# Linear attention and a mixture of experts in one kernel: the issue order of SyncE's loads, GpSimd's transfers and two groups of TensorE work

## The chip, the cores and the metric

The kernel runs on one core of one Trainium2 chip. The metric is the device time of one execution in microseconds (us), as the median of several runs. A core has five engines, each with its own instruction queue that it works through in order: TensorE (PE; its weight loads are shown as PEld), VectorE (DVE), ScalarE (ACT), GpSimd (POOL) and SyncE (SP, which only issues transfers here). Transfers issued by SyncE and by GpSimd run on the core's 16 DMA engines.

## The reference, cut to what matters

```
x: [4, 2048, 256], so 8192 tokens of 256
xn = layernorm(x)
# attention: 8 heads, keys of 128, values of 64, a gated linear recurrence
q, k, v = xn Wq, xn Wk / sqrt(128), xn Wv
alpha   = sigmoid((xn Wg + bg) / 16)            # one per token and head
state   = alpha * state + outer(k, v)           # over the tokens of a sequence
att     = ((q . state) * sigmoid(xn Wog)) Wo
# experts: 64, of which each token takes 8, at most 256 tokens an expert
scores  = sigmoid(xn gate_w^T)
groups  = the best 4 of 8 groups of 8 experts, by their two best (scores + bias)
top 8   = the best 8 experts in them; weights = 2.5 * scores / their sum
buf[e]  = the first 256 tokens that chose e
y       = (silu(buf w_gate) * (buf w_up)) w_down            # for each expert
ffn     = for each token the weighted sum of its experts' y
out     = x + att + ffn
```

## The kernel before

The work has two strands that are interleaved on all engines.

**Attention** runs over 32 blocks of 256 tokens (`block(s)`). Every product is made of three half-precision products of high and low parts (`product`, L253 to L257: high x high, high x low, low x high). A block loads its transposed tokens `xs`, its decay rows `aj` and `mv` and its decay factors `el` (`load_block`, `load_el`), all one block ahead. It projects them (`project`, tile `pj`: `queries`, `keys`, `values`, `gate`), splits the results into parts on ScalarE (L206) and VectorE (L207), and has the keys of four heads at a time transposed by a DMA from SyncE (`kt`, L841, two of them in a block). `unit_a` makes the scores and decays `sp` and `dc`, `unit_m` multiplies them (L874), `unit_d` makes outputs and the new state (`od`, which reads `kt`), `output` multiplies by Wo, and `finish(s - 1)` adds the block before to the output: by one accumulating transfer from GpSimd (L940), and for the last two blocks through SyncE: read, add on VectorE, write (L945 to L948).

**The experts' strand** first routes: 16 batches of 512 tokens. `front` normalizes them, stores them, has them transposed (`xT`, L366, a DMA from SyncE on what GpSimd leaves at L363), and four calls later makes the logits `lg` (L378 to L382). `back` chooses the experts and counts. When all batches are routed (about 605 us), the experts begin, at 5 for each 12 steps of the attention:

- `steps(g)` loads the counts of NF experts (`c`, L557) and subtracts them (L560), and `find` makes of them the row numbers `idx` of an expert's 256 tokens, three experts ahead;
- `fetch(e)` loads the expert's weights `w` (three transfers of 128 KB from SyncE, L589 to L591) and gathers its tokens `xe` (two indirect transfers from GpSimd, L594);
- `expert_in` transposes the tokens on TensorE (`xet`, L607) and splits weights (`wh` on ScalarE, L611, `wl` on VectorE, L679) and tokens;
- `expert_mid` makes `gu`, `expert_out` makes `yp` and `y` (L651);
- `expert_add` adds `y` to the output rows (two indirect accumulating transfers from GpSimd, L665). Each waits until the last two additions, or a block's finish between them, have landed (`behind_adds`).

```
        new = owed[0] >= 1.0                      # at 5 of 12 steps
        ...
    for it in list(q):                            # expert_step: every expert in flight, one stage on
        expert_stages[st](e, m)
    ...
    moe["at"].append([e, fetch(e), 0])            # then the next expert's transfers
```

So an expert is gathered in one period (2.4 steps) and transposed in the next; its additions are written in the fourth period after its gather, just ahead of the gather of the expert four later. `block` calls `step()` 12 times, in the last block 7 times, 379 in all; the experts begin at the 205th step, and the last of the 64 gathers is written at about the 358th.

**What sets the order.** The source order is not the issue order. The kernel is compiled with a scheduler that gives each engine the instruction it holds to be ready first, and the earlier written among several; it estimates for itself how long transfers take. The order is fixed in the program, so an engine that comes to an instruction too early waits. `tc.issue_after(ins)` puts what is written in its block behind `ins` in the queue of the same engine; it orders the issue alone and waits for nothing.

## Time and profile before

| | |
|---|---|
| median of 3 runs | 1246.25 us (1245.57 to 1248.66) |
| profiled execution | 1258.39 us, of which its span is 1256.6 us |
| granted TensorE clock, mean | 0.982 |
| TensorE busy, 60 to 560 us (routing and attention) | 466.4 of 500 us |
| TensorE busy, 600 to 1240 us (experts and attention) | 602.9 of 640 us |
| DMA, mean over the span | 162 GB/s |

The profile is of one execution. Its page gives the busy time of each engine, then groups of instructions by line, engine and tile; tiles are named as in the kernel, `out<-in`. A row of a waits view reads "engine, line waited for, what ended the wait: us in total, times, longest". A row of a timeline gives start, duration, engine, line, operation, count, and in brackets the engine's idle time before it and what ended that. SPq is SyncE issuing a transfer; the time beside it is that of the issue, not of the transfer. The chain is the work that ended last, followed back to the start; a DMA piece in it runs from issue to landing.

### The profile page before, as it was taken

Reading aid. Unit: us, or ns where it says so; the run is one execution under the profiler, and the core shown is the slowest. Engines: PE = TensorE matmul, PEld = TensorE weight load, DVE = VectorE, ACT = ScalarE, POOL = GpSimd, SP = SyncE. Lnnn points to the kernel's source line nnn. Section 1 sums busy time; section 2 is a strip of 40 time slices with the busy share of each in tenths; the row PEclk is TensorE's granted clock in tenths of the full one; section 3 lists DMA queues with packets and bytes.
Section 4 is the critical chain, followed back from the end, with each engine's and each line's share of the span. In section 5 each row is a group of like instructions: output and inputs, shape, how many; then the busy total and the mean of one; then the engine's idle time right before and its main releaser. Section 6 shows DMA issues by size and latency. Waiting matters only on the chain.

```text
span 1256.6 us, 32315 instructions
## 1 busy us (share of the span) xinstructions
PE 1146.2 (91%) x12421; PEld 961.1 (76%) x12421; DVE 960.6 (76%) x2685; ACT 754.4 (60%) x1455; POOL 740.5 (59%) x961
## 2 busy tenths in 40 slices
PE   3697999999999989998999999899889999999898
PEld 2576777877777767787887888788678888787686
DVE  7986777777676767777898788787768889787676
ACT  4566666756665656655566566565556666565564
POOL 4376777665777767552356466655467566564651
PEclk9998999999999999999999999899989999999899
DMA  7649878777777776648689797898778797998854
GB/s 234 197 93 254 196 177 179 166 186 167 176 173 153 174 143 138 157 94 192 128 178 156 158 189 146 163 181 159 144 162 166 175 178 161 155 172 161 142 77 85
DMA packets 313498, 203.74 MB, mean 162 GB/s; under 512 B 198528, under 2 KB 283648, under 8 KB 313088
## 3 DMA queue, kind: packets, MB, share of 16 engines
q1 hardware_dynamic: 280608, 156.05, 53.2%
q0 software_dynamic: 32736, 45.63, 22.9%
q8 instruction: 97, 1.59, 0.5%
q14 instruction: 57, 0.47, 0.1%
HBM read 112.57 MB, written 54.71 MB: 133 GB/s over the span
## 4 chain that ended last, share of the span: by engine, by line
PE 48%; DMA 19%; DVE 12%; POOL 10%; issue 6%; ACT 4%; SPq 1%; POOLq 0%; DVEq 0%; ACTq 0%
PE pj L257 8%; PE pj L255 8%; PE pj L256 8%; DMA xe<-xw_d,idx 7%; DMA xT<-x 4%; PE od L891 3%; DMA el<-el_d 3%; PE od L895 3%; DMA kt<-k 2%; PE xet L607 2%; PE gu L255 2%; PE gu L256 2%; PE gu L257 2%; POOL out_dram L665 1%; DVE qt L822 1%
## 5 line engine op out<-in xcount | busy, mean ns | idle before, releaser
L665 POOL DMA_INDIRECT out_dram<-y,idx x128 | 210.3, 1643 | 207.0 <-ACT y L651 40.1
L594 POOL DMA_INDIRECT xe<-xw_d,idx x128 | 136.8, 1068 | 49.2 <-issue 32.3
L257 PE MATMUL pj<-xs,wk_l 128*128 128x256 f16 x496 | 135.6, 273 | 0.0
L255 PE MATMUL pj<-xs,wk_h 128*128 128x256 f16 x496 | 135.4, 273 | 0.0
L256 PE MATMUL pj<-xs,wk_h 128*128 128x256 f16 x496 | 135.3, 273 | 0.0
L256 PE MATMUL pj<-xs,wq_h 128*128 128x256 f16 x496 | 135.3, 273 | 0.0
L257 PE MATMUL pj<-xs,wq_l 128*128 128x256 f16 x496 | 135.2, 273 | 0.0
L255 PE MATMUL pj<-xs,wq_h 128*128 128x256 f16 x496 | 135.2, 273 | 0.0
L874 DVE TENSOR_TENSOR dc<-sp,dc 128x512 f32<-128x512 f32 x128 | 87.7, 685 | 57.3 <-POOL dc L861 49.8
L891 PE MATMUL od<-dc,v 128*64 128x128 f32 x1024 | 112.9, 291 | 9.5 <-DVE dc L874 8.4
L207 DVE SCALAR_TENSOR_TENSOR ql<-pj,qh 128x512 f16<-128x512 f32 x128 | 87.2, 681 | 39.4 <-ACT qh L206 39.1
L206 ACT ACTIVATE qh<-pj 128x512 f16<-128x512 f32 x128 | 76.3, 596 | 48.9 <-PE pj L257 48.5
L895 PE MATMUL od<-qt,state 128*64 128x128 f32 x960 | 103.4, 279 | 0.0
L255 PE MATMUL sp<-qh,k 128*128 128x128 f16 x512 | 96.5, 221 | 0.2 <-ACT k L206 0.2
L206 ACT ACTIVATE k<-pj 128x512 f16<-128x512 f32 x128 | 76.0, 594 | 34.4 <-PE pj L257 33.9
L256 PE MATMUL sp<-ql,k 128*128 128x128 f16 x512 | 96.1, 220 | 0.0
L257 PE MATMUL sp<-qh,k 128*128 128x128 f16 x512 | 95.5, 220 | 0.0
L855 ACT ACTIVATE dc<-lp 128x512 f32<-128x512 f32 x128 | 76.6, 599 | 28.4 <-PE lp L851 27.8
L207 DVE SCALAR_TENSOR_TENSOR k<-pj,k 128x512 f16<-128x512 f32 x128 | 86.9, 679 | 8.2 <-ACT k L206 7.9
L891 PEld LDWEIGHTS od<-dc,v 128*64 128x64 f32 x1024 | 62.0, 138 | 39.7 <-DVE dc L874 11.8
L822 DVE SCALAR_TENSOR_TENSOR qt<-pj,el 128x512 f32<-128x512 f32 x128 | 86.7, 678 | 2.1 <-DMA el<-el_d 2.1
L679 DVE TENSOR_TENSOR wl<-w,wh 128x768 fp32r<-128x768 f32 x64 | 61.1, 955 | 35.0 <-ACT wh L611 33.9
(397 smaller groups left out, 4282.9 us busy)
## 6 DMA issues: line engine op xcount, KB each, us to landing
el<-el_d SPq DMA_DIRECT2D x64, 512.0 KB
xw_d<-x SPq DMA_DIRECT2D x16, 512.0 KB
xT_d<-xT SPq DMA_DIRECT2D x16, 512.0 KB
out_dram<-in_L_attn_x_dram SPq DMA_DIRECT2D x16, 512.0 KB
w<-in_L_ffn_w_gate_dram SPq DMA_DIRECT2D x64, 128.0 KB
w<-in_L_ffn_w_up_dram SPq DMA_DIRECT2D x64, 128.0 KB
w<-in_L_ffn_w_down_dram SPq DMA_DIRECT2D x64, 128.0 KB
xs<-xT_d SPq DMA_DIRECT2D x31, 256.0 KB
```

Of the source, the lines that this page charges most:

```text
L206: return (nc.scalar.activation(hi, t, AF.Copy, scale=scale).ins, nc.vector.scalar_tensor_tensor(lo, in0=t, scalar=scale, in1=hi, op0=ALU.m ...
L207: nc.vector.scalar_tensor_tensor(lo, in0=t, scalar=scale, in1=hi, op0=ALU.mult, op1=ALU.subtract).ins)
L255: nc.tensor.matmul(out_, lhsT=a[0], rhs=b[0], start=first, stop=False)
L256: nc.tensor.matmul(out_, lhsT=a[0], rhs=b[1], start=False, stop=False)
L257: return nc.tensor.matmul(out_, lhsT=a[1], rhs=b[0], start=False, stop=last).ins
L594: nc.gpsimd.indirect_dma_start(out=xe[:, f, :], out_offset=None, in_=xw_d[:, :], in_offset=bass.IndirectOffsetOnAxis(ap=idx[:, e, f:f + 1] ...
L665: two = [nc.gpsimd.indirect_dma_start(out=of, out_offset=bass.IndirectOffsetOnAxis(ap=idx[:, e, f:f + 1], axis=0), in_=m["y"][:, f, :], in ...
L822: read = nc.vector.scalar_tensor_tensor(qt, in0=pj, scalar=QFIT, in1=two_heads(el, i), op0=ALU.mult, op1=ALU.mult)
L855: nc.scalar.activation(dc, lp, AF.Relu, scale=-1.0)
L874: anchor.append(nc.vector.tensor_tensor(dc, B["sp"], dc, ALU.mult).ins)
L891: nc.tensor.matmul(op[i * DV:(i + 1) * DV, j, :], lhsT=v[:, h0 + 2 * j + i, :], rhs=dc[:, 2 * j + i, :], start=True, stop=first)
L895: nc.tensor.matmul(op[i * DV:(i + 1) * DV, j, :], lhsT=state[half][:, 2 * j + i, :], rhs=qt[:, ck, 2 * j + i, :], start=False, stop=True)
```

## The change

- `steps`, the weights of an expert, `load_block` and `load_el` issue their SyncE transfers behind the last key transposition written so far (`behind_keys`).
- GpSimd's gathers, additions and block finishes are issued in the order in which they are written (`in_turn`).
- The logits and the experts' token transposes are issued behind the last projection written so far (`behind_projections`).
- An expert's weights become a stage of their own between gather and transposes. So the transposes and all later stages of an expert come one period later after its gather, with five token buffers in place of four.
- NF is 4 in place of 8: counts are loaded for four experts at a time.
- The last block but one is added to the output by GpSimd's accumulating transfer, like those before it.

```diff
--- before.py
+++ after.py
@@ -53,7 +53,7 @@
 DGROUPS = ((0, 1), (1, 1), (2, 2), (4, 4), (8, 4), (12, 4))
 
 STEPS = 12
-NF = 8
+NF = 4
 AHEAD = 2
 EXPERTS = 5
 
@@ -297,6 +297,10 @@
     zs = r1.tile([P, NB, H, RT], F32, name="zs")
     sg = r1.tile([P, NB, H, RT], F32, name="sg")
     batch = {}
+
+    def behind_projections():
+
+        return tc.issue_after(made["pj"]) if "pj" in made else ExitStack()
 
     def load_x(b):
         rows = slice(b * RB, (b + 1) * RB)
@@ -376,10 +380,11 @@
         for _ in range(3 if b > 2 else 1):
             yield True
         lg = ps["mo"].tile([P, RT, E + H], F32, tag="mo", name="lg")
-        for t in range(RT):
-            for c in range(2):
-                made["lg"] = product(lg[:, t, :], (xT[:, t, 0, c, :], xT[:, t, 1, c, :]),
-                                     (gwz[:, 0, c, :], gwz[:, 1, c, :]), c == 0, c == 1)
+        with behind_projections():
+            for t in range(RT):
+                for c in range(2):
+                    made["lg"] = product(lg[:, t, :], (xT[:, t, 0, c, :], xT[:, t, 1, c, :]),
+                                         (gwz[:, 0, c, :], gwz[:, 1, c, :]), c == 0, c == 1)
         nc.vector.scalar_tensor_tensor(zs[:, b].rearrange("p h t -> p t h"), in0=lg[:, :, E:E + H],
                                        scalar=unfit[:, WG:WG + 1], in1=bc(brow, 1, RT),
                                        op0=ALU.mult, op1=ALU.add)
@@ -549,13 +554,24 @@
 
     moe = {}
 
+    def in_turn(issue):
+
+        with tc.issue_after(moe["turn"]) if "turn" in moe else ExitStack():
+            moe["turn"] = issue().ins
+        return moe["turn"]
+
+    def behind_keys():
+
+        return tc.issue_after(made["kt"]) if "kt" in made else ExitStack()
+
     def steps(g):
 
         both = []
         for t in range(2):
             c = moe["m1"].tile([NTL, NF, P], F16, name=f"c{t}")
-            nc.sync.dma_start(out=c, in_=cnt_d[t * E:(t + NTL) * E, :].rearrange(
-                "(t e) i -> t e i", e=E)[:, g * NF:(g + 1) * NF, :])
+            with behind_keys():
+                nc.sync.dma_start(out=c, in_=cnt_d[t * E:(t + NTL) * E, :].rearrange(
+                    "(t e) i -> t e i", e=E)[:, g * NF:(g + 1) * NF, :])
             both.append(c)
         nc.vector.tensor_tensor(dd_t[g % 2][0:NTL, :, 0:P], both[1], both[0], ALU.subtract)
 
@@ -584,27 +600,31 @@
             find(e)
 
     def fetch(e):
-        w4 = moe["w4"]
-        w = w4.tile([P, 6, I], F32, name="w", bufs=3)
-        nc.sync.dma_start(out=w[:, 0:2], in_=w_gate[e].rearrange("(c p) i -> p c i", p=P))
-        nc.sync.dma_start(out=w[:, 2:4], in_=w_up[e].rearrange("(c p) i -> p c i", p=P))
-        nc.sync.dma_start(out=w[:, 4:6].rearrange("p c i -> p (c i)"), in_=w_down[e])
-        xe = w4.tile([P, 2, XW], F32, name="xe", bufs=4)
+        xe = moe["w4"].tile([P, 2, XW], F32, name="xe", bufs=5)
         for f in range(2):
-            nc.gpsimd.indirect_dma_start(
+            in_turn(lambda: nc.gpsimd.indirect_dma_start(
                 out=xe[:, f, :], out_offset=None, in_=xw_d[:, :],
-                in_offset=bass.IndirectOffsetOnAxis(ap=idx[:, e, f:f + 1], axis=0))
-        return dict(w=w, xe=xe)
+                in_offset=bass.IndirectOffsetOnAxis(ap=idx[:, e, f:f + 1], axis=0)))
+        return dict(xe=xe)
+
+    def expert_weights(e, m):
+        w = moe["w4"].tile([P, 6, I], F32, name="w", bufs=3)
+        with behind_keys():
+            nc.sync.dma_start(out=w[:, 0:2], in_=w_gate[e].rearrange("(c p) i -> p c i", p=P))
+            nc.sync.dma_start(out=w[:, 2:4], in_=w_up[e].rearrange("(c p) i -> p c i", p=P))
+            nc.sync.dma_start(out=w[:, 4:6].rearrange("p c i -> p (c i)"), in_=w_down[e])
+        m["w"] = w
 
     def expert_in(e, m):
 
         xt = ps["mo"].tile([P, 2, 2, 2, P], F16, tag="mo", name="xet")
-        for f in range(2):
-            rows = m["xe"][:, f, 0:D].bitcast(F16)
-            for a in range(2):
-                for c in range(2):
-                    k = (2 * a + c) * P
-                    nc.tensor.transpose(xt[:, a, c, f, :], rows[:, k:k + P], identh)
+        with behind_projections():
+            for f in range(2):
+                rows = m["xe"][:, f, 0:D].bitcast(F16)
+                for a in range(2):
+                    for c in range(2):
+                        k = (2 * a + c) * P
+                        nc.tensor.transpose(xt[:, a, c, f, :], rows[:, k:k + P], identh)
         w3, m1 = moe["w3"], moe["m1"]
         wh = w3.tile([P, 6, I], F32R, name="wh")
         wl = w3.tile([P, 6, I], F32R, name="wl")
@@ -662,16 +682,16 @@
     def expert_add(e, m):
 
 
-        two = [nc.gpsimd.indirect_dma_start(
+        two = [in_turn(lambda: nc.gpsimd.indirect_dma_start(
             out=of, out_offset=bass.IndirectOffsetOnAxis(ap=idx[:, e, f:f + 1], axis=0),
             in_=m["y"][:, f, :], in_offset=None, compute_op=ALU.add,
-            bounds_check=NT - 1, oob_is_err=False).ins for f in range(2)]
+            bounds_check=NT - 1, oob_is_err=False)) for f in range(2)]
         for ins in two:
             behind_adds(ins)
         tc.declare_no_dep(two[1], two[0], reason="the halves of an expert share no row")
         adds.extend(two)
 
-    expert_stages = [expert_in, expert_mid, expert_out, expert_add]
+    expert_stages = [expert_weights, expert_in, expert_mid, expert_out, expert_add]
 
     def expert_late():
 
@@ -688,7 +708,7 @@
             if st == len(expert_stages):
                 continue
             expert_stages[st](e, m)
-            if st == 1:
+            if st == 2:
                 mids.append((e, m))
             it[2] += 1
         for e, m in mids:
@@ -838,7 +858,7 @@
         split(two_heads(k[:, :, 0], i), two_heads(k[:, :, 1], i), pj, DK ** -0.5 * KFIT)
         if i == 1:
             kt = ktp.tile([P, NCK * 2 * 4, P], F16, name="kt")
-            nc.sync.dma_start(out=kt, in_=k.rearrange("p c a h t -> p (c a h t)"), transpose=True)
+            made["kt"] = nc.sync.dma_start(out=kt, in_=k.rearrange("p c a h t -> p (c a h t)"), transpose=True).ins
             B["kt"][half] = kt
 
     def unit_a(s, half, ck):
@@ -936,9 +956,9 @@
     def finish(s):
         res = blk[s]["res"]
         rows = slice(s * S, (s + 1) * S)
-        if s < NS - 2:
-            behind_adds(nc.gpsimd.dma_start(out=of[rows, :].rearrange("(t p) d -> p t d", p=P), in_=res,
-                                            accum_op=ALU.add).ins)
+        if s < NS - 1:
+            behind_adds(in_turn(lambda: nc.gpsimd.dma_start(
+                out=of[rows, :].rearrange("(t p) d -> p t d", p=P), in_=res, accum_op=ALU.add)))
         else:
             mo = xsp.tile([P, NCK, D], F32, tag="xs", name="mo")
             dst = of[rows, :].rearrange("(t p) d -> p t d", p=P)
@@ -953,8 +973,9 @@
 
         n = s + 1 < NS
         if n:
-            load_block(s + 1)
-            load_el(s + 1, 0)
+            with behind_keys():
+                load_block(s + 1)
+                load_el(s + 1, 0)
         unit_a(s, 0, 0)
         if n:
             queries(s, 1, 0)
@@ -984,7 +1005,8 @@
         else:
             queries(s, 1, 1)
         if n:
-            load_el(s + 1, 1)
+            with behind_keys():
+                load_el(s + 1, 1)
             gate(s + 1, 0)
         step()
         unit_d(s, 0, 1)
```

## The prediction

> **What bounds the kernel now.** I read the page first, then TensorE's waits, the busy times by stage, and the timelines of GpSimd and SyncE around the worst waits. The page, core 0:
>
> ```profile
> PE 1146.2 (91%) x12421; PEld 961.1 (76%) x12421; DVE 960.6 (76%) x2685; ACT 754.4 (60%) x1455; POOL 740.5 (59%) x961
> ```
>
> TensorE works 91% of 1256.6 us; no other engine passes 76%. So a change gains only what it takes from TensorE's 110 us of idle time, and from matmuls run at a lowered clock. Who ends the idle time (in total, times, longest, us):
>
> ```profile
> PE xet L607 <- DMA xe<-xw_d,idx: 33.4, 22, 7.2
> PE lg L255 <- DMA xT<-x: 31.1, 15, 9.8
> PE tot L171 <- ACT junk L155: 9.3, 1, 9.3
> PE od L891 <- DVE dc L874: 8.4, 9, 3.2
> PE od L255 <- DMA kt<-k: 4.5, 3, 2.8
> ```
>
> Two rows hold 64.5 us: the token transposes of an expert wait for gathered rows (expert phase, from 605 us), and the logits for transposed tokens (routing phase). From 60 us on the second is 20.9 us in 13 waits; the rest is start-up, which the change leaves alone. Transposed keys, by contrast, are waited for three times. What a long wait leaves behind, by stretch (length, PE busy, PEld, DVE, ACT, POOL, PEclk, DMA share, GB/s):
>
> ```profile
> 803.00:812.00 9.00, 6.35 (x63) 5.16 (x64) 3.02 (x12) 2.32 (x4) 6.47 (x6) 0.62 0.58 104
> 907.00:914.00 7.00, 0.00 (x0) 0.00 (x0) 1.91 (x5) 0.19 (x1) 5.11 (x4) 0.65 0.59 139
> 914.00:920.00 6.00, 5.30 (x23) 3.09 (x23) 1.72 (x4) 1.81 (x4) 4.69 (x4) 0.55 0.53 77
> ```
>
> TensorE stands still for 7 us, then works at 0.55 of its clock. How the worst wait came about, GpSimd's timeline and then TensorE's:
>
> ```profile
> 885.75 0.95 POOL L594 DMA_INDIRECT xe<-xw_d,idx  x1 [0.30 <-issue]
> 888.09 1.40 POOL L940 DMA_DIRECT2D out_dram<-res  x1
> 898.51 1.65 POOL L665 DMA_INDIRECT out_dram<-y,idx  x1 [9.02 <-DMA out_dram<-res]
> 907.24 1.55 POOL L665 DMA_INDIRECT out_dram<-y,idx  x1 [5.21 <-ACT hs L628]
> 910.96 1.02 POOL L594 DMA_INDIRECT xe<-xw_d,idx  x1 [0.30 <-issue]
> 912.28 0.98 POOL L594 DMA_INDIRECT xe<-xw_d,idx  x1 [0.30 <-issue]
> ...
> 914.19 0.61 PE L607 MATMUL xet<-identh,xe 128*128 128x128 f16 x4 [7.24 <-DMA xe<-xw_d,idx]
> ```
>
> One gather was pulled ahead of the finish of a block (L940); the next then came only behind that finish and two experts' additions, each of which waits for the landing before it: 25 us between gathers instead of 9.4 (64 experts' gathers start over 605.9 to 1202.9). TensorE reached the transposes 2 us after the second gather was issued. SyncE, with the chain's piece for its last line:
>
> ```profile
> 1059.67 0.37 SPq L764 DMA_DIRECT2D el<-el_d  x1
> 1061.29 0.34 SPq L740 DMA_DIRECT2D xs<-xT_d  x1
> 1061.76 0.37 SPq L589 DMA_DIRECT2D w<-in_L_ffn_w_gate_dram  x1
> 1063.29 5.29 SPq L841 DMA_TRANSPOSE kt<-k  x1
> ...
> 1063.29 13.29 DMA kt<-k
> ```
>
> Loads that nobody needs for another 15 us or more stand right ahead of a key transposition, which then takes 13.29 us against 6.13 and 7.51 elsewhere on the chain.
>
> **The change, part by part.**
>
> *A period later.* An expert's gather is now followed by a step for its weights, and only then by its transposes. One period is 597/63.5 = 9.4 us. The longest wait for a gather is 7.2 us, so one more period covers every one of the 22. This holds if the compiled order really sets the transposes a period further from their gather: in the trace they come 1 to 38 us after the last projection written ahead of them (only the first expert's come before it), so it is the scheduler's estimate of the gather, not the source, that places them. With four experts in flight, an expert's additions (which stand ahead of the gather four later) come about 34 us after its gather (981 to 1015), or 8.5 us an expert: just about the period, which is why the experts fall ever further behind the attention. With five in flight the same 34 us is 6.8 an expert, and the source position can rule. I take four fifths of the 33.4: -27, and keep 6 for gathers behind a block's finish. Bounds: 0 and -33.
>
> *The clock.* After the waits of 2.6, 4.1, 7.2 and 5.1 us at 690, 805, 914 and 1167 the granted clock was 0.76, 0.62, 0.55 and 0.59 over 7, 9, 6 and 6 us, with 6.8, 6.4, 5.3 and 5.6 us of busy time: lost 0.24 x 6.8 + 0.38 x 6.4 + 0.45 x 5.3 + 0.41 x 5.6 = 8.7 us. The Trainium skill ("TensorE: Matmul & The Clock Gate", "What's actually happening") has half clock follow an idle window of about 3.4 us and last about as long; that would price three waits at 1.7 each, 5 us. The trace shows a wait of 2.6 us doing it too, so I use 8.7, with the same four fifths: -7.
>
> *GpSimd in program order.* No instruction is added; the few gathers that now stand ahead of a finish or of earlier additions (646, 691, 886 and 1129 us among them) fall behind these. Such a gather is then issued up to 9.0 us (wait for the finish) plus two additions of 1.6 later. Of two periods' lead, 18.8 us, some 6 are left, against gathers of 3 to 10 us on the chain: that is the 6 us kept above. In exchange no 25 us hole follows. Queued behind are only other transfers: in this phase GpSimd computes nothing. The last-but-one block's finish goes from SyncE (0.38 + 2 x 0.36 us of issue, two VectorE additions of 0.42) to one GpSimd issue of 1.3, before the end and beside TensorE: 0.
>
> *Loads behind the last keys.* Nothing is added but their wait. They are moved past kt, and whatever is moved past it runs later: per block two el, xs, two aj, two mv, and five experts' w (three transfers each) and c. The gain: kt has the rings to itself; od's waits for it are 4.5 us in all, so at most -4. The price: what is late next. xs and el are read half a block (15 us and more) later, against 5.29 of issue and landings of 4 to 9 us; covered. The weights are the closest: written one period, 9.4 us, before ScalarE copies them (wh), and five experts against two key transpositions a block means 2 of 5, or 26, are written just behind one. The skill ("DMA: Bandwidth & Descriptors", "Two DMAs through the same engine are not ordered") says descriptors of a queue start in order: weights begin only behind kt, which speaks against this change. In the trace the three loads issued at 1070.90 behind the kt of 13.29 landed by 1077.43, 0.85 us after it and 14.1 us after its issue. By that slow kt a load would come 4.7 us late, 26 of them 122 us; by one of 7.5, 8.4 us, which is in time. By the rule without overlap (7.5 plus the 2.81 us of a w piece on the chain) it would be 0.9 late. Since kt loses the traffic ahead of it, I take the ordinary kt and +2 (bounds 0 and +122).
>
> *Logits behind the last projection.* All 15 later lg already stand 0 to 26 us behind it, so this edge moves none. What can move is xT. GpSimd waited for el before L363, which makes xT's input, 3.81 us at 229.81 (L828); that el is now issued elsewhere. Against it, the block's second el is now written next to xT. Between -20.9 and +20 (13 el pieces of 4.4 us, a third of each seen) I take -4, close to the row of kt's traffic.
>
> *Smaller steps.* NF 4: 16 more c issues of 0.52 us on SyncE and 8 more subtractions of 0.34 to 0.67 on VectorE (at most 5 us of 300 idle): 0 while VectorE stays at 76%.
>
> *The end.* Now the experts, trailing, fill TensorE until 1226:
>
> ```profile
> 560.00:600.00 40.00, 36.75 (x382) 29.61 (x382) 30.94 (x70) 21.31 (x41) 8.85 (x11) 0.96 0.66 153
> 1200.00:1240.00 40.00, 40.00 (x424) 33.96 (x424) 26.39 (x55) 22.97 (x46) 17.07 (x12) 1.00 0.59 88
> 1240.00:1257.00 17.00, 10.84 (x129) 9.08 (x126) 10.42 (x20) 5.56 (x11) 0.00 (x0) 1.00 0.24 62
> ```
>
> If they no longer trail, the last 17 of 379 steps run attention alone, some 45 us as in the first row, which loses 3.25 in 40; the last block without filler loses a little more. +5 (0 to +12).
>
> Sum: -27 - 7 - 4 + 2 + 5 = -31. The profiled execution took 1258.39 us (its span and 1.8 around it), 1% over the median of 1246.25; -31 leaves 1227 there, 1215 against the median.
>
> **The rivals.** *Just in time again.* If the scheduler goes on placing the transposes by its own estimate, they move up with their gathers and the waits stay; so would they if GpSimd's fixed order cost what the period gives. For: the order by estimate above. Against: five experts in flight. Then -5 instead of -27 and no clock gain: -5 - 4 + 2 + 5 = -2, 1244.
>
> *Weights too late (slower).* ScalarE reaches wh before the weights have landed and holds the casts of qh, k and xeh behind it, on which TensorE's buffers hang. Halfway between in time and the slow kt's 4.7, 2.4 us at each of 26 is +62: 1277. It decides from 31/26 = 1.2 us an expert on. For: kt at 13.29, and a DMA share of 0.9 at 1080 to 1120. Against: today ScalarE waits for w 5.0 us in all (three waits), and it idles 40%.
>
> **How the numbers follow.** Gain as summed: 0.58, own range 1198 to 1235. Just in time: 0.17 (0.08 faster, 0.07 same, 0.02 slower). Late weights: 0.25, 1250 to 1280. Below 0.3% (3.7 us) a measurement of this kernel can't tell a change from none. Faster 0.66, same 0.07, slower 0.27. The range: 1194 takes in most of the logits' 21 us; 1266 takes in half of the late weights; about 0.05 and 0.11 are left out.
>
> **What would show it.** Right: xet's wait for xe below 10 us; no clock under 0.9 in 40 us stretches after 605; about 9.4 us between gathers; kt pieces under 9 us; the last experts' additions ending before 1200. Wrong: xet still at 25 us or more (first rival), or ScalarE's wh waiting for w above 30 us and pj or gu among TensorE's waits (second), or lg's wait above 31.

## The result: slower by 3%

The changed kernel takes 1286.39 us (median of 4 runs, 1284.07 to 1298.42), against 1247.45 us of the kernel before on the same chip (4 runs, 1245.57 to 1256.32): ratio 1.0317, 95% interval 1.0236 to 1.0399. The forecast was 1215 us. A ratio here compares means of runs on the same chip without those more than 1.5% above the fastest of their kernel, so it can exceed the quotient of the medians, by up to 0.6% in most rows below and by 1.4% for e27, where 7 of 11 runs of the kernel before are left out. The profiled execution took 1287.55 us (span 1285.8), against 1258.39 before. The page, core 0:

```profile
PE 1157.5 (90%) x12421; PEld 969.7 (75%) x12421; DVE 958.4 (75%) x2691; ACT 753.2 (59%) x1454; POOL 750.4 (58%) x962
```

TensorE does the same 12421 matmuls and is busy 11 us longer; its idle time grew from 110 to 128 us. The two make up the 29 us between the profiled spans. The first is the clock: in both traces TensorE's granted clock is either 1.00 or 0.50, and it stood at 0.50 for 44 us before and 69 us after. What ends the idle time (TensorE's waits, the whole span):

```profile
PE lg L255 <- DMA xT<-x: 31.5, 12, 9.8
PE pj L255 <- DVE qt L842: 11.9, 6, 3.2
PE od L255 <- DMA kt<-k: 11.6, 2, 10.6
...
PE xet L627 <- DVE idx L594: 11.3, 3, 5.3
...
PE row L587 <- DVE dd L576: 6.7, 4, 2.5
```

The row that led before, `xet <- DMA xe` with 33.4 us, is gone. In its place stand waits for things that come from SyncE: row numbers and differences of counts (`idx` and `dd`, both made from `c`), and one wait of 10.6 us for transposed keys. VectorE's and ScalarE's waits show the same loads from the other side:

```profile
DVE dd L576 <- DMA c<-cnt_d: 47.0, 12, 7.0
```

```profile
ACT wh L631 <- DMA w<-in_L_ffn_w_down_dram: 22.4, 12, 4.7
```

GpSimd did what was forecast of it. Its timeline at a block's finish, where a gather once ran ahead and left a hole of 25 us:

```profile
907.39 1.01 POOL L605 DMA_INDIRECT xe<-xw_d,idx  x1 [0.30 <-issue]
908.71 1.60 POOL L605 DMA_INDIRECT xe<-xw_d,idx  x1 [0.30 <-issue]
911.00 1.37 POOL L960 DMA_DIRECT2D out_dram<-res  x1 [0.69 <-ACT dc L876]
915.62 1.76 POOL L685 DMA_INDIRECT out_dram<-y,idx  x1 [3.25 <-DMA out_dram<-res]
917.68 1.58 POOL L685 DMA_INDIRECT out_dram<-y,idx  x1 [0.30 <-DVE hs L651]
919.57 1.03 POOL L605 DMA_INDIRECT xe<-xw_d,idx  x1 [0.31 <-PE pj L257]
```

The next gather is 12 us later, and the wait for the finish to land is 3.25 us of that. From an expert's second gather to its transposes there are 17.4 us on the mean of experts 8 to 59, before 8.1.

**Where the 29 us went.** The first key transposition of a block is a good milestone: SyncE issues 64 of them, two a block. Their times in the two profiled executions, and the end of TensorE's work, with TensorE's idle time in each stretch and what half the clock cost it (half of its busy time at 0.50), before and after:

| stretch | before | after | difference | idle | half clock |
|---|---|---|---|---|---|
| start to block 16 (routing) | 569.9 | 585.1 | +15.2 | 64.3, 70.0 | 3.6, 15.9 |
| block 16 to block 19 (the experts begin) | 108.6 | 119.5 | +10.9 | 3.7, 13.1 | 1.5, 3.1 |
| block 19 to block 30 (experts) | 508.2 | 498.2 | -10.0 | 35.9, 27.3 | 10.2, 7.7 |
| block 30 to TensorE's last matmul | 66.2 | 79.1 | +12.9 | 2.8, 14.0 | 0.0, 2.2 |

So a third of the forecast gain is there, in the middle; three losses stand around it. The first is more clock than waiting, the other two are waits. SyncE stands long at key transpositions in all three. Its timeline where the experts begin:

```profile
599.68 1.00 SPq L784 DMA_DIRECT2D el<-el_d  x1
611.25 1.81 SPq L861 DMA_TRANSPOSE kt<-k  x1
613.11 1.76 SPq L573 DMA_DIRECT2D c<-cnt_d  x2
...
619.33 0.44 SPq L613 DMA_DIRECT2D w<-in_L_ffn_w_gate_dram  x1
```

From 600.7 to 611.25 SyncE issues nothing: the transposition waits for its keys, and the counts, a block's loads and weights stand behind it. The first counts go out at 613.11. In the kernel before they go out some 40 us earlier:

```profile
568.70 0.52 SPq L557 DMA_DIRECT2D c<-cnt_d  x1
573.60 0.58 SPq L557 DMA_DIRECT2D c<-cnt_d  x1
```

The first gather is at 623.4, before at 605.9. At the end:

```profile
1253.12 0.38 SPq L965 DMA_DIRECT2D mo<-out_dram  x1
1253.60 9.57 SPq L861 DMA_TRANSPOSE kt<-k  x2
```

The last block's read of the output (L965) waits for the last additions, and here it stands ahead of the last two key transpositions. TensorE waits 10.6 us for them. SyncE's wait there:

```profile
SPq L965 <- DMA out_dram<-y,idx: 20.0, 1, 20.0
```

Busy times by stage of the kernel after (length, PE busy, PEld, DVE, ACT, POOL, PEclk, DMA share, GB/s):

```profile
60.00:560.00 500.00, 458.08 (x5125) 374.14 (x5122) 348.37 (x1090) 308.79 (x558) 338.42 (x629) 0.97 0.68 162
1240.00:1286.00 46.00, 29.32 (x311) 24.90 (x308) 21.10 (x41) 13.98 (x26) 9.41 (x6) 0.88 0.44 58
1258.00:1268.00 10.00, 4.48 (x32) 4.12 (x33) 0.75 (x2) 0.82 (x2) 0.23 (x1) 0.50 0.87 106
1268.00:1272.00 4.00, 4.00 (x48) 3.47 (x47) 2.94 (x5) 2.27 (x5) 0.98 (x1) 1.00 0.54 70
```

In routing (first row) TensorE is busy 458.1 us of 500 and does 5125 matmuls, before 466.4 us and 5307. The last two rows are what goes with the wait of 10.6 us: half the clock from 1257.7, within the wait, until 1267.9, 4.4 us after it. And SyncE's waits in routing:

```profile
SPq L861 <- DVE state L934: 55.6, 8, 11.8
...
SPq L861 <- DVE oT L924: 24.1, 3, 13.7
SPq L861 <- DVE gs L479: 21.4, 3, 11.5
```

L861 is the key transposition; the names behind the arrow are VectorE's instructions nearest to the event. All its rows of this view (60 to 560 us) sum to 201.6 us, called "SyncE at keys" below; the same sum before is 106.9. SyncE does not stand longer for that. All rows of the view, for all its instructions, sum to 343 us before and 348 after, and to 335 to 358 in every run below. Before, much of it was spent at a block's own loads, L740 (`xs`) and L764 (`el`):

```profile
SPq L740 <- PE pj L257: 43.1, 11, 8.9
SPq L841 <- DVE state L914: 28.3, 6, 13.8
SPq L764 <- DVE qt L822: 28.2, 7, 6.4
```

So the number says which instruction heads SyncE's queue, not how much time is lost.

### The profile page after: what moved, and what is told of

It reads as the page before. It is cut to its first block, busy times and chain, and to the rows that moved or that the text cites. A ratio compares the mean times of both kernels' runs of the same rounds, so it can differ in the third digit from the quotient of the medians.

```text
span 1285.8 us, 32158 instructions
## 1 busy us (share of the span) xinstructions
PE 1157.5 (90%) x12421; PEld 969.7 (75%) x12421; DVE 958.4 (75%) x2691; ACT 753.2 (59%) x1454; POOL 750.4 (58%) x962
## 4 chain that ended last, share of the span: by engine, by line
PE 46%; DMA 17%; DVE 15%; POOL 7%; issue 5%; ACT 5%; SPq 4%; another core or an unknown queue 1%; DVEq 0%; POOLq 0%; ACTq 0%
PE pj L257 8%; PE pj L255 8%; PE pj L256 8%; DMA xT<-x 5%; DMA el<-el_d 4%; PE od L911 3%; DMA c<-cnt_d 3%; PE od L915 2%; DVE wl L699 2%; PE gu L255 2%; PE xet L627 1%; PE gu L257 1%; PE gu L256 1%; DMA w<-in_L_ffn_w_down_dram 1%; DMA kt<-k 1%
## 5 line engine op out<-in xcount | busy, mean ns | idle before, releaser
L685 POOL DMA_INDIRECT out_dram<-y,idx x128 | 216.0, 1688 | 182.2 <-ACT y L671 37.0
L605 POOL DMA_INDIRECT xe<-xw_d,idx x128 | 137.6, 1075 | 57.8 <-issue 31.5
L255 PE MATMUL pj<-xs,wk_h 128*128 128x256 f16 x496 | 137.6, 277 | 6.5 <-DVE qt L842 5.9
L256 PE MATMUL pj<-xs,wk_h 128*128 128x256 f16 x496 | 137.6, 277 | 0.0
L255 PE MATMUL sp<-qh,k 128*128 128x128 f16 x512 | 98.4, 224 | 4.7 <-ACT k L206 4.7
L257 PE MATMUL sp<-qh,k 128*128 128x128 f16 x512 | 97.4, 224 | 1.8 <-DVE k L207 1.3
L924 DVE SCALAR_TENSOR_TENSOR oT<-og,od 128x256 f32<-128x256 f32 x128 | 53.0, 414 | 52.7 <-PE od L257 43.1
```

Source lines behind the costliest of these rows:

```text
L255: nc.tensor.matmul(out_, lhsT=a[0], rhs=b[0], start=first, stop=False)
L256: nc.tensor.matmul(out_, lhsT=a[0], rhs=b[1], start=False, stop=False)
L257: return nc.tensor.matmul(out_, lhsT=a[1], rhs=b[0], start=False, stop=last).ins
L605: in_turn(lambda: nc.gpsimd.indirect_dma_start(out=xe[:, f, :], out_offset=None, in_=xw_d[:, :], in_offset=bass.IndirectOffsetOnAxis(ap=id ...
L685: two = [in_turn(lambda: nc.gpsimd.indirect_dma_start(out=of, out_offset=bass.IndirectOffsetOnAxis(ap=idx[:, e, f:f + 1], axis=0), in_=m[" ...
```

## The experiments

All are edits of the changed kernel unless said otherwise. A ratio compares with runs of the kernel before on the same chip. "Key 33" is the issue of block 16's first key transposition, in us. A profile is one execution, and executions of one kernel differ: the kernel before ran from 1227 to 1266 us. Where two programs have the same order on every engine until block 16, "key 33" still differs by up to 8.5 us (e16 and e27). Differences of 9 us in it are not read.

| run | the keys rule holds for | other differences | median us | ratio, 95% | key 33 | SyncE at keys |
|---|---|---|---|---|---|---|
| change | all | | 1286.39 | 1.0317 [1.0236, 1.0399] | 585.1 | 201.6 |
| e11_keys_only | all | before, with this rule alone | 1280.15 | 1.0321 [1.0226, 1.0416] | 587.5 | 194.3 |
| e1_no_keys | nothing | | 1250.57 | 1.0056 [1.0022, 1.0089] | 570.3 | 111.1 |
| e3_mo_last | all | last read behind keys | 1269.53 | 1.0187 [1.0115, 1.0258] | 583.5 | 196.6 |
| e2_c_free | all but c | | 1273.87 | 1.0222 [1.0142, 1.0302] | 586.1 | 200.4 |
| e4_blocks_free | c, w | | 1261.44 | 1.0138 [1.0103, 1.0173] | 562.6 | 106.6 |
| e15_pair | el, xs, aj, mv | | 1259.84 | 1.0140 [1.0083, 1.0197] | 584.1 | 199.4 |
| e27_el_free | all but el | | 1254.36 | 1.0196 [1.0118, 1.0275] | 566.4 | 129.6 |
| e13_el_only | el | | 1247.37 | 1.0054 [1.0029, 1.0080] | 578.2 | 137.0 |
| e14_xs_only | xs, aj, mv | | 1238.61 | 0.9962 [0.9930, 0.9993] | 561.0 | 126.4 |
| e16_xs_mo | xs, aj, mv | last read behind keys | 1240.52 | 0.9957 [0.9918, 0.9995] | 557.9 | 134.2 |
| e12_w_only | w | last read behind keys | 1241.13 | 0.9991 [0.9953, 1.0029] | 569.1 | 110.4 |

### Is it the keys rule?

e1_no_keys takes the rule out of the change; e11_keys_only puts it alone into the kernel before.

```diff
     def behind_keys():
-        return tc.issue_after(made["kt"]) if "kt" in made else ExitStack()
+        return ExitStack()
```

> The whole change but for the rule that SyncE's loads go behind the last transposed keys. Theory (the rule is the loss: late block loads in the routing phase +16, late counts at the start of the experts +14, SyncE held by the last block's read +12, against -14 in between): all 42 us of loss go, and 1286 becomes 1215 to 1245, under the kernel before. First rival (the loss comes from the experts being a period later and GpSimd's fixed order, whatever SyncE does): it stays within 5 us of 1286. Second rival (the compiled order simply falls out differently with any edit): between the two, with the waits in new places.

> The kernel before with the keys' rule alone (NF 8, four buffers, an expert transposed one period after its gather, GpSimd's order and TensorE's order free, the last two blocks finished through SyncE). Theory (the rule itself costs 36 us, whatever stands beside it): 1270 to 1290. Rival (it costs so much only together with the weights' own stage and the counts for four experts): below 1260.

Taking it out gives back 2.6% (1.0317 to 1.0056), and alone it costs 3.2%. Both agree, so the rule is worth some +35 us wherever it stands. The rest of the change is about nothing in sum: its theory had e1 at 1215 to 1245, under the kernel before, and it did not come there. The prediction had put its late loads at +2. Both edits redraw the order of all engines, not SyncE's alone, so this is the price of the rule as it is compiled.

### Which loads, and where?

One class of loads is freed in the change (e2: c; e4: all of a block; e27: el), or the read at the end is moved (e3).

```diff
-            behind_adds(nc.sync.dma_start(out=mo, in_=dst).ins)
+            with tc.issue_after(made["kt"]):
+                behind_adds(nc.sync.dma_start(out=mo, in_=dst).ins)
```

> The change, with the last block's read of the output (mo, which waits for the last additions) put behind the last transposed keys on SyncE. Theory (SyncE stood at mo and the last two key transpositions behind it): TensorE's wait of 10.6 us for kt goes, and the time falls by 10 to 12, to about 1275. Rival (the tail is long because the experts end 20 us later, and the keys merely show it): within 4 us of 1286.

SyncE's timeline at its end:

```profile
1238.32 9.09 SPq L861 DMA_TRANSPOSE kt<-k  x2
1250.69 0.38 SPq L966 DMA_DIRECT2D mo<-out_dram  x1
```

With the read behind them the transpositions go out 15 us earlier. From block 30 to the end there are 64.3 us (change 79.1, before 66.2), and 17 us are gone from the median. VectorE's, ScalarE's and GpSimd's orders are those of the change, TensorE's but for 4 of 12421 places, and SyncE's differs in nothing else: the loss at the end is this one place in the queue.

```diff
-            with behind_keys():
+            with ExitStack():
                 nc.sync.dma_start(out=c, in_=cnt_d[t * E:(t + NTL) * E, :].rearrange(
```

> The change, with only the count loads c left free to go ahead of the keys. Theory: VectorE's 47 us of waiting for c go, the first gather moves from 623 to about 610, TensorE's idle time in blocks 17 to 19 falls from 18 to under 6 us, and the time falls by 10 to 18 to about 1272. Rival (c is hidden, TensorE's idle there is the normal filling of a longer pipeline): within 4 us of 1286.

VectorE's waits with free counts:

```profile
DVE dd L576 <- DMA c<-cnt_d: 4.9, 2, 2.9
```

The wait of 47.0 us for counts is 4.9, TensorE's 18.0 us of waits for `idx` and `dd` are gone, blocks 16 to 19 take 112.4 us (change 119.5, before 108.6), and 12.5 us are gone from the median. (The first gather moves only to 618.8, not to the theory's 610.) At the same time `xet <- DMA xe` is back, with 17.6 us in 13 waits. So its absence in the change was no pure gain: the experts' strand was held by its counts, which gave the gathers time.

What the rule does to a load can be read as its lead, the time from its issue (the last piece's) to the start of its first reader (means in us; `el` and `xs` from 60 to 560 us):

| load, first reader | without the rule (e1) | with it (change) |
|---|---|---|
| `el`, VectorE's `qt` | 39.1 | 17.9 |
| `xs`, TensorE's `pj` of the gate | 31.8 | 9.8 |
| `w`, ScalarE's `wh` | 25.1 | 10.2 |
| `c`, VectorE's `dd` | 30.0 | 4.9 |

Free, a load runs far ahead of its place in the source; under the rule it comes where it is written. Counts are written just ahead of their use, so they are late.

```diff
-            with behind_keys():
+            with ExitStack():
                 load_block(s + 1)
                 load_el(s + 1, 0)
 ...
-            with behind_keys():
+            with ExitStack():
                 load_el(s + 1, 1)
```

> The change, with the block loads (xs, aj, mv, el) left free and only c and the weights behind the keys. Theory (late block loads cost the 16 us by which block 15 starts later): block 15 starts at 541 as before, not 557, and the time falls by 12 to 18 to about 1271. Rival (the routing phase is slower for another reason, such as the logits' rule): block 15 still at about 557, within 4 us of 1286.

25 us are gone, and in the profiled execution block 16 comes 22.5 us earlier: the routing phase is lost with the block's own loads. The three parts (17, 12.5 and 25 us) sum to 54, more than the 36 that the whole rule gives, so they are no shares of it. Which of a block's loads it is was tried by letting the rule hold for el alone, for xs, aj and mv alone, and for both, with c and w free (that is, `load_el` or `load_block` or both inside the `with`):

> The change with only the el loads behind the keys; xs, aj, mv, c and the weights are free. Theory (of the block loads it is the 512 KB el, 9 us and more from issue to use by VectorE and GpSimd, that is late): the start of block 15 moves to about 553 and the time is some 12 above that without the rule, about 1262. Rival (it is xs, on which the next block's projections hang): block 15 at 541 or earlier, within 5 of 1250.

> The change with only xs, aj and mv behind the keys; el, c and the weights are free. Theory (el is what is late): block 15 at 541 or earlier, within 5 of 1250. Rival (xs is late for the projections that fill TensorE in the second half of a block): block 15 at 550 or later, 1260 or more.

> Change with the rule kept for all of a block's loads (xs, aj, mv and both el) and lifted for the counts c and the weights w. Theory (the routing phase is lost only where tokens and decay factors are late together): block 15 starts at 552 us or later, as in the change (557), and the time is about 1262. Rival (the block loads cost nothing by themselves; the 25 us that went when they were freed came from their standing in one row with c and w): block 15 at 540 or earlier, as with each alone, and about 1243. In the routing phase there are no c or w loads, so by the rival block 15's start of 557 would have been variation between executions.

el alone brings block 16 to 578.2, some 8 us late, and costs nothing in the end (1.0054, without the rule 1.0056; blocks 19 to 30 take 478.7 us): its theory had the delay and missed the time. xs, aj and mv alone bring it to 561.0, not late at all, and the kernel becomes slightly faster than before. Both together bring it to 584.1, as in the change, and the time to 1259.84 us, near the theory's 1262: beside xs, el costs 1.8% (0.9962 to 1.0140). The last test frees el alone in the full change:

```diff
             with behind_keys():
                 load_block(s + 1)
-                load_el(s + 1, 0)
+            load_el(s + 1, 0)
 ...
-            with behind_keys():
+            with ExitStack():
                 load_el(s + 1, 1)
```

> The change with the decay factors el free and all else of it kept (xs, aj, mv, c and w behind the keys). Theory (el carries the routing loss): the 33rd key transposition, at the start of block 16, issued at 556 to 566 us as against 585.1 in the change, SyncE's standing at key transpositions from 60 to 560 us 130 us or less (201.6), ratio about 1.014 as with all block loads free. Rival (only the row of all loads does it): 575 us or later, and 1.025 or more.

Its busy times in routing, and a row of SyncE's waits there:

```profile
60.00:560.00 500.00, 473.63 (x5329) 386.40 (x5328) 360.66 (x1135) 316.33 (x573) 344.31 (x638) 0.98 0.71 167
```

```profile
SPq L861 <- DVE state L934: 35.1, 7, 6.4
```

TensorE does 5329 matmuls in the 500 us, as against 5125, and SyncE's standing at keys falls to 129.6 us. So the routing loss hangs on el beside xs. The two orders with both under the rule (e11, and the change, which e2, e3 and e15 share until block 16) reach block 16 at 583 to 588; the seven other orders without el under it at 558 to 572. The time decides less: by the ratio (1.0196) it lies between what the two theories gave, by the medians it is 1.0061. The profiled execution keeps the loss at the end (75.7 us from block 30 on), but not the one at the experts' start (108.2 us).

The table's last column falls in three groups: 107 to 111 us where no block load is under the rule, 126 to 137 with one of the two kinds, 194 to 202 with both. With nothing left that may go ahead, SyncE comes to the transposition early, and all that is written behind it stands still with it. Yet neither is late: in the change el lands within 7.5 us of its issue and VectorE first reads it 13.3 us after the issue or later; for xs it is 3.6 and 6.9 us. GpSimd's wait for el is not longer either (`wall`: 34.9 us in routing, before 40.7). Why TensorE loses is only partly seen. Its logits wait 21 to 25 us for xT in routing where el is under the rule, 11 to 16 in the changed kernels where it is not (before 20.9), and ScalarE waits longer for GpSimd's `nb` (37.4 us, before 28.6), on which the next batch's xT hangs. But all orders change with such an edit, and no run here holds the other engines' orders while el moves. That cause stays open.

Weights alone, with the read at the end moved:

> Change with the rule kept for the weights w alone, counts and all block loads free, and the last read of the output behind the last key transposition. Theory (weights are not what is late; block loads, counts and the end are): 1236 to 1248, ScalarE's wh waits for w below 15 us. Rival (late weights, the prediction's second rival): 1258 or more, wh waits for w 20 us or more.

ScalarE's waits in that run:

```profile
ACT wh L631 <- DMA w<-in_L_ffn_w_down_dram: 20.8, 5, 5.4
ACT wh L631 <- DMA w<-in_L_ffn_w_up_dram: 2.9, 2, 2.2
ACT wh L631 <- DMA w<-in_L_ffn_w_gate_dram: 2.3, 1, 2.3
```

26 us of waits for weights, as many as in the change (22.4 and 4.6), and the time is that of before: late weights cost nothing that shows. The moved read could hide a few us; in e16 below it gave nothing. With free counts (e2) ScalarE waits even longer, and that kernel is faster than the change:

```profile
ACT wh L631 <- DMA w<-in_L_ffn_w_down_dram: 39.9, 15, 5.0
```

The rival expectation had the wait right and its price wrong.

### What is the rest worth?

| run | kernel | median us | ratio, 95% |
|---|---|---|---|
| e18_turn_only | before, GpSimd's order alone | 1256.38 | 1.0050 [1.0016, 1.0085] |
| e19_proj_only | before, logits and token transposes behind projections alone | 1254.84 | 1.0042 [1.0012, 1.0073] |
| e23_nf4_only | before, NF 4 alone | 1259.73 | 1.0081 [1.0054, 1.0108] |
| e17_no_period | change without keys rule and period | 1273.30 | 1.0243 [1.0162, 1.0325] |
| e10_period | change without keys rule and both orders | 1265.61 | 1.0215 [1.0142, 1.0287] |
| e1_no_keys | change without keys rule | 1250.57 | 1.0056 [1.0022, 1.0089] |
| e24_nf8 | e1, NF 8, last read behind keys | 1259.85 | 1.0152 [1.0088, 1.0216] |
| e25_nf8_xs | e24, xs, aj, mv behind keys | 1240.28 | 0.9957 [0.9924, 0.9990] |

e10_period keeps the period, its fifth buffer and NF 4, and takes out both order rules, and the keys rule as in e1:

```diff
-        with tc.issue_after(moe["turn"]) if "turn" in moe else ExitStack():
+        with ExitStack():
 ...
-        return tc.issue_after(made["pj"]) if "pj" in made else ExitStack()
+        return ExitStack()
```

> Of the change only the period, with its five buffers, NF 4 and the last block's finish on GpSimd: no keys' rule, GpSimd's order free, no projections' rule. Theory (the longer pipeline gives its period to the gather's own queueing, not to the transposes: gather to addition grows from 36 to about 44 us, second gather to transposes stays at 8): TensorE's wait for xe stays at 20 us or more, and the time is 1240 to 1252, as without the keys' rule alone. Rival (GpSimd's fixed order eats what the period gives): the wait for xe falls under 10 us and the time to 1225 or less.

It was slower than forecast, and its wait for xe is 27.3 us. e17_no_period goes the other way, with the two order rules and without the period (four buffers again):

```diff
-    expert_stages = [expert_weights, expert_in, expert_mid, expert_out, expert_add]
+    expert_stages = [expert_in, expert_mid, expert_out, expert_add]
 ...
-            moe["at"].append([e, fetch(e), 0])
+            m = fetch(e)
+            expert_weights(e, m)
+            moe["at"].append([e, m, 0])
```

> Change without the rule on the keys and without the extra period: weights are loaded with the gather, four token buffers, transposes in the next period. GpSimd's order, the logits' and token transposes' edge, NF 4 and the last-but-one finish stay. Theory (the period only lengthens the loop from gather to addition and leaves the wait as it was; GpSimd's order is what helps): 1238 to 1250, xet waits for xe 20 to 33 us, fetch to add 34 to 38 us. Rival (the prediction's step, a period more lead is what shortens that wait): 1258 or more, with xet waiting over 33 us.

That theory fell in its time. With the orders held, the kernel with the period is 1.9% faster (1.0243 to 1.0056, some 23 us, near the -27 of the prediction). Without them it is slower: 1.0215 with the period (and NF 4), 1.0081 with NF 4 alone. TensorE's wait for gathered rows, e17 and then e1:

```profile
PE xet L627 <- DMA xe<-xw_d,idx: 31.8, 20, 4.4
```

```profile
PE xet L627 <- DMA xe<-xw_d,idx: 25.4, 19, 3.4
```

The wait itself hardly shrinks. Behind the last projection written ahead of it, a gather comes after 15.0 us without the period and 22.9 with it, the transposes after 14.0 and 13.9; from the second gather to the transposes it is 6.9 and 8.3 us. The gathers moved 8 us later and took the period's lead with them. What the 23 us come from was not found, and a redrawn order is not excluded.

If the period gives 23 and the sum is +7, something that had been put at 0 costs about 30. The three parts were tried alone, on the kernel before:

```diff
-            nc.gpsimd.indirect_dma_start(
+            in_turn(lambda: nc.gpsimd.indirect_dma_start(
 ...
-        for t in range(RT):
+        with behind_projections():
+            for t in range(RT):
 ...
-NF = 8
+NF = 4
```

> Kernel before with GpSimd's transfers in program order and nothing else; all other engines' queues are those of before. Theory A (GpSimd's order without the period takes lead from the gathers, and that is the 30 us hidden in the sum): 1265 to 1280, xet waits for xe 40 us or more. Theory B (it removes the 25 us holes between gathers and is a gain by itself, NF 4 being what costs): 1230 to 1243, xet's longest wait under 5 us. The prediction's step said 0.

> Kernel before with the logits and the token transposes behind the last projection and nothing else. The prediction's step said that it moves nothing, -4 at most: 1242 to 1249. Rival (token transposes were sometimes taken ahead of a projection and are now held): 1255 or more.

> Kernel before with NF 4 in place of 8: counts loaded for four experts at a time, 16 loads more, each of half the size. Theory B (the counts' loads are what was costed at nothing and costs: the experts' order changes, idx comes later, SyncE has more loads ahead of the weights): 1265 to 1280, with row or xet waiting for counts. Theory A: 1244 to 1252.

None of the theories holds: each part costs a little. The three sum to +1.7%, inside the interval of e17, which has them all (and the last-but-one finish). GpSimd's order alone is the cleanest of all runs, since every other engine's queue is, instruction for instruction, that of before. TensorE's waits there:

```profile
PE xet L627 <- DMA xe<-xw_d,idx: 22.8, 17, 5.0
```

The wait falls by 10.6 us and its longest from 7.2 to 5.0 us, and the kernel is 0.5% slower. Last, NF 8 with the period: the second counts are loaded into the tile of the difference, which makes the room that NF 4 had made.

```diff
-            c = moe["m1"].tile([NTL, NF, P], F16, name=f"c{t}")
+            c = dd_t[g % 2][0:NTL, :, 0:P] if t else moe["m1"].tile([NTL, NF, P], F16, name="c0")
```

> Change without the keys rule, with NF 8 (the second counts are loaded into the tile of the difference and subtracted in place) and the last read of the output behind the last key transposition. If the costs add (no keys 1.0056, less 0.008 for NF 4): ratio 0.997, 1243. If NF 4's cost came only from another drawing of the whole order: no better than 1.0056, 1253.

> As the run before, and with the keys rule on a block's tokens and decay rows (xs, aj, mv) alone. If the costs add (0.9957, less 0.008): ratio 0.988, 1235, faster than both kernels. Else about 0.996, as with NF 4.

The costs do not add: e24 is 1% slower than e1, e25 equals e16. So NF 4's +0.8% is no fixed price of smaller loads: beside the period the kernel with NF 4 (e1) is the faster. Each such edit redraws the whole compiled order, and that seems to move the time by about 1% either way.

> Change with the rule kept for a block's tokens and decay rows alone (xs, aj, mv), and with the last block's read of the output written behind the last key transposition. Theory (what stands behind a key transposition at the end costs 12 to 17 us wherever the read stays in front): the last block takes 22 us as before, 1228 to 1234, faster than the kernel before by 1%. Rival (the end is already short in this version, since fewer experts trail): 1236 to 1241, as without the second edit.

e14, e16 and e25 (tokens and decay rows behind the keys, all else free) are the best: 0.9957 to 0.9962 of before, each with an interval just under 1. The second edit of e16 gave nothing there: its theory fell, the rival held.

## Why the prediction was wrong, step by step

- **Loads behind the last keys: +2 taken, bounds 0 and +122; measured about +35.** This step failed. It reckoned a load's delay as the time of a transposition's transfer and looked for the price at the weights, which cost nothing that shows (e12, e2). For c it counted 16 issues of 0.52 us, not its lead, which fell from 30.0 to 4.9 us: VectorE waits 47.0 us for counts, and freeing them gave 12.5 us. It did not ask what the last transpositions stand behind: 17 us (e3). Of "xs and el ... covered" the reading was right, both land before they are read; the conclusion was not, since el under the rule beside xs goes with some 19 us in routing (585.1 to 566.4, e27), and how it costs them stays open. The Trainium skill ("DMA: Bandwidth & Descriptors", "Two DMAs through the same engine are not ordered"), which the step weighed, says that descriptors of a queue start in order but are pipelined; the prediction's own lines agree, with weights landing 0.85 us after the kt ahead of them. The losses seen here arise a stage earlier, in the issuing engine (600.7 to 611.25 us, no issue at all).
- **kt itself: -4 at most.** As argued: its mean from issue to landing fell from 6.9 to 5.7 us, and od's wait for it from 4.5 to 1.0 us, but for the 10.6 us by the queue at the end.
- **A period later: -27.** The wait that it was to remove stays at 25.4 us without the keys rule, as the first rival said; in the change it is gone because counts hold the experts back (with c free it is 17.6). The -23 between e17 and e1 is near the forecast by luck: it does not come from that wait, and without the two orders it does not come at all.
- **The clock: -7; measured +11.** TensorE is busy 11 us longer for the same matmuls; the mean granted clock fell from 0.982 to 0.973. New waits took the place of the old. (The 0.76 and 0.62 of the forecast are means of stretches in which the clock was first 0.50 and then 1.00; its sum stands.)
- **GpSimd's order, the logits' edge, NF 4: 0, -4, 0; measured +0.5, +0.4 and +0.8% alone.** The logits still wait 31.5 us (before 31.1).
- **The end: +5; measured +12.9 in the profiled executions**, by L965 ahead of the last kt. The prediction counted what experts no longer fill.
- **The signs.** Most of those that were to show it right came: no wait of xet for xe, gathers 9.4 us apart, and until the last wait no clock under 0.9 in stretches of 40 us (0.91 at least) and no kt of 9 us. Only the last experts' additions came at 1248.5, not before 1200. The kernel was slower all the same: the signs watched the old loss, not new ones.
- **Rivals.** "Weights too late" came near the time (1277; its own terms give 1275, since the +2 is counted twice) by a mechanism that is not there: w's waits of 27 us stay under its mark of 30, and 39.9 us in e2 cost nothing that shows. "Just in time again" describes e1.

## What to carry to other kernels

A rule that puts loads behind an instruction ends their running ahead: it sets them back to where they are written, and to that instruction's own wait. Before costing it by transfer times, compare each load's lead with what the source leaves it (counts: 30 us, then 5), and look at the last instance of the rule, where nothing follows that could hide it. What is written well ahead of its use stood it here (tokens and decay rows: -0.4% against before). What is used at once did not (counts). Decay factors stood it alone, but not beside the tokens. A queue's standing time at one instruction is no measure of loss as long as its total stays the same (343 and 348 us). Where a compiler draws the order, small edits moved the time by up to 1%, so a gain of that size has to be tried alone, and costs found alone need not add.

## What was not expected of the hardware

- A transfer that waits in SyncE's queue holds everything behind it: the read of 0.38 us at 1253.12 kept two key transpositions, and with them TensorE, for 10.6 us.
- The clock fell within that wait, at 1257.7, and came back at 1267.9, 4.4 us after TensorE had resumed: half of the 4.48 us busy in 1258 to 1268 is 2.2 us lost, on top of the wait.
- One order, two executions: e16 and e27 have the same queues until block 16 and the same idle time there (54 and 55 us). They reach it at 557.9 and 566.4, after 3 and 24 us at half clock.
